# Two mixture-of-experts layers in two halves of the batch, with the state space layer of one half beside the expert tiles of the other

## The chip, the cores and the metric

The kernel runs on one core of one Trainium2 chip. The core has a matrix engine (PE, whose weight loads the profile lists apart as PEld), three engines for the rest of the arithmetic (DVE, ACT, POOL), and SP, which here only issues DMAs. Each engine works through its own instructions in order, and waits where an instruction needs a result that another engine or a DMA has not delivered. The time is device microseconds (us) of one execution.

## The reference

The input `x` holds 4 sequences of 512 tokens with 128 features in f32, 2048 tokens in all. Four layers follow one another, and each is added to its input and normalized over the features:

```
x = layernorm(x + attention(x))    # 16 heads of 8; token t sees t-64 .. t+64
x = layernorm(x + moe0(x))         # shared expert, and the best 2 of 12 experts by softmax weights
x = layernorm(x + ssm(x))          # state space layer
x = layernorm(x + moe1(x))         # the best 2 of 8 experts
```

An expert of `moe0` computes `(a * gelu(g)) @ We2 + be2` with `a, g = split(x @ We1 + be1)`, 384 wide. An expert of `moe1` computes `gelu(x @ w1 + b1) @ w2 + b2`, 512 wide, adds `x`, and applies a layernorm with a gamma and a beta of its own before it is weighted.

The state space layer projects a token to z and x (256 each, 4 heads of 64), B and C (64 each, normalized), and small numbers per head. B and C are turned by a phase that is a running sum over time. Per head a state of 64 x 64 runs over the 512 steps: `h = d[t] * h + input[t]`, with a decay `d` per step and an input made of x and B of this and the step before; `y = C h + D x`; the output is `(y * silu(z)) @ W_out`.

## The kernel before

**Memory and order.** Tiles are 128 tokens (P = 128), so a sequence has NT = 4 of them, and NB = 4 is the number of sequences. Buffers come from pools: a tile with a tag and `bufs=6` has six buffers in turn, and a seventh user waits until the first is free. The order of instructions on each engine is chosen by the framework's scheduler from the program's order and its own estimates; inside `as_written("PE")` PE keeps the order of the program text. Before, only attention stands in such a block.

**Attention** (lines 490 to 800). PE goes through the scores and the products with the values of all four sequences, one after the other. When a sequence's sums are done, a generator, a "chain", takes it on: `attention_out`, then `moe0_shared` (the shared expert, the gates and the top two of 12) and `route`. A part of each chain runs per attention step. The loop goes on until the chains are empty.

**Routing** (lines 303 to 505). The table in DRAM is the core of both expert layers. `route_table` allots one region of NB·T = 2048 rows per expert and fills it with zeros (12 DMAs of 1 MB). `route` gives each token of a sequence its rank within its experts, by matmuls that count, and POOL puts each token's row into the table by indirect DMAs (L363), 8 per sequence and layer, 128 rows each. `route_end` waits for the counts of all four sequences and computes from them which rows and which expert each tile has. With two experts per token and regions that end in a part of a tile, a loop needs a fixed number of tiles:

```
tiles = 2 * NB * T // P + n - 1        # n = 12: 43 tiles; n = 8: 39 tiles
```

`route_regs` loads these numbers into registers for eight tiles at a time. `tiles` (L477) is a pipeline written out by hand; in step t stand the load of tile t+3, the turn of t+1, the up projection of t and the down projection of t−1:

```
for t in range(-3, n + 1):
    if t + 3 < n:          s[t + 3] = load(r, t + 3)
    if 0 <= t + 1 < n:     self.route_turn(r, t + 1, s[t + 1])
    if 0 <= t < n:         up(r, t, s[t])
    if 0 <= t - 1:         down(r, t - 1, s.pop(t - 1))
```

A load is two DMAs on SP and one POOL copy: the tile's rows from the table into `io` (L452, 64 KB; six buffers), the expert's up weights (L453; four buffers), the expert's bias (L456). The turn is a transposition on PE (L462) and a copy on ACT (L463). In `moe0` the up projection is six matmuls (L859), Gelu on ACT (L867) and a product on DVE (L868); the down projection is three matmuls (L471), a DVE copy into `io` (L875) and a store on SP into a second DRAM table, `ys` (L876). In `moe1` POOL adds a vector to the rows (L1266), PE does four matmuls up (L1271), ACT the Gelu (L1274), PE four down, DVE the residual and the layernorm (L1281 to L1289), and SP a store (L1290). A row load, a tile's result and its store share one `io` buffer.

`route_back` gathers, for one sequence, two result rows per token: 8 indirect DMAs on POOL (L498) of 128 rows each. `moe0_back` and `moe1_back` weight and add them and normalize.

**State space layer** (lines 890 to 1230). After the first tile loop, `moe0_back` and `ssm_project` run per sequence, then `ssm_weights` for all 16 tiles together. Time goes in 16 chunks of 128 tokens (4 sequences of 4). `chunk_matrix` computes each chunk's decays between any two of its steps: a DVE product, one f32 matmul of 512 columns (pe, L1126), an exponential on ACT (L1128) and a POOL product (L1129), and scales x three ways on ACT (L1141). `chunk_outputs` adds what the chunk's own inputs give (py) and what the state carries in, and renews the state (pst). `chunk_out` turns y on PE (pyt) and multiplies by W_out. When a sequence is done, its gates and puts for the second layer (`moe1_gates`) run behind the chunks of the next.

**The order of the stages**, from `tile_kernel` (L1314), is: attention, tiles of `moe0`, state space layer, tiles of `moe1`, `moe1_back`. Each stage has pools of its own that close when it ends.

Of the kernel before, what the change touches and what calls it, by code (L numbers as in the profile page):

```python
# [20 lines left out]
D = 128  # L21

# [14 lines left out]
class Kernel:  # L37
# [47 lines left out]
    def consts(self):  # L85
# [48 lines left out]
        nc.vector.tensor_scalar(self.first_row, self.tile_no[:, :16], float(NB * T), None, ALU.mult)  # L134
# [63 lines left out]
    def weights_moe1(self):  # L198
# [6 lines left out]
        for i, name in enumerate(("b2", "gamma")):  # L205
            at = 4 + i * D
            nc.gpsimd.dma_start(
                out=self.u1[:, :, at : at + D], in_=d[name].partition_broadcast(P)
            )
        self.down = self.const.tile([P, NE0 * 3, D], F32, tag="down", name="down1")  # L210
# [91 lines left out]
    def route_table(self):  # L302

        nc = self.nc
        self.table = self.dram.tile([NE0 * NB * T, D], F32, name="table")
        zero = self.const.tile([P, D], F32, tag="zero", name="zero")
        nc.gpsimd.memset(zero, 0.0)
        m = NB * T // P
        for e in range(NE0):
            nc.sync.dma_start(  # L310
                out=self.table[e * NB * T : (e + 1) * NB * T, :].rearrange("(p m) d -> p m d", m=m),
                in_=zero[:, None, :].to_broadcast([P, m, D]),
            )


    def route_start(self, n, name, width, down, bias):
# [3 lines left out]
        tiles = 2 * NB * T // P + n - 1  # L320
# [3 lines left out]
            "n": n, "name": name, "tiles": tiles, "down": down, "bias": bias, "reg": {}, "count": count, "batch": [], "puts": [], "y": {},  # L324
            "ys": self.dram.tile([tiles * P, width], F32, name=f"ys_{name}"),
        }

    def route(self, r, b, x, hots):
# [29 lines left out]
        r["batch"].append((hots, rank))  # L358
        place = self.placed(hots, rank, self.first_row[:, :n], n, "put")
        for i in range(NT):  # L360
            yield
            for k in range(2):
                put = nc.gpsimd.indirect_dma_start(  # L363
                    out=self.table, out_offset=bass.IndirectOffsetOnAxis(ap=place[:, k, i : i + 1], axis=0),
# [20 lines left out]
    def route_end(self, r):  # L385
# [14 lines left out]
        done = self.s2.tile(shape, F32, tag="done", name=f"done{n}", bufs=1)  # L400
# [4 lines left out]
        ex = self.small([P, 64], "ex", 1)[:, :tiles]  # L405
        nc.vector.tensor_reduce(ex, done, AX.X, ALU.add)
        nc.vector.tensor_tensor(done, done, t0[:, None, :].to_broadcast(shape), ALU.mult)
        off = self.small([P, 64], "off", 1)[:, :tiles]
# [3 lines left out]
        table = self.sm.tile([P, 4, 64], I32, tag="table", name="table", bufs=1)  # L412
        nc.vector.scalar_tensor_tensor(
            off, ex, float(NB * T // P), off, ALU.mult, ALU.add
# [3 lines left out]
            table[:, 0, :tiles], off, float(P), float(n * NB * T - P), ALU.mult, ALU.min  # L418
# [5 lines left out]
        r["table"] = table  # L424
# [971 lines left out]
```

## Time and profile before

| | |
|---|---|
| time, median of 14 runs | 840.2 us (836.53 to 848.72) |
| time of the profiled execution | 841.62 us |
| its span, first to last instruction | 839.9 us |
| mean granted PE clock | 0.796 |
| busy: PE | 578.4 us (69%), 3852 matmuls |
| busy: PEld | 402.1 us (48%) |
| busy: DVE | 391.8 us (47%), 1331 instructions |
| busy: ACT | 327.9 us (39%), 861 |
| busy: POOL | 316.4 us (38%), 454 |
| moved by DMA | 68.73 MB, mean 82 GB/s |

Busy times overlap, since the engines run side by side; no engine is busy all the time. The granted clock is the share of full speed at which PE was allowed to run. The span leaves out 1.7 us of the time, around the first and the last instruction.

The chain that ended last, followed back from the last instruction, is by engine: PE 46%, DMA 14%, DVE 12%, ACT 8%, POOL 8%, issue 8%. Its costliest lines are short shares of many stages: `io_b<-table` 5%, `pse` (L687) 4%, `io_a<-table` 4%, `psc` (L658), `table` (L363), `pg` (L859), `py` (L1161), `pe` (L1126) and `ph` (L1271) 3% each. So an average over the span tells little, and the time has to be read stage by stage.

### The profile page before, as it was taken

What the parts mean: (1) busy time and instruction counts of PE and PEld (TensorE: products, weight loads), DVE (VectorE), ACT (ScalarE), POOL (GpSimd) and SP (SyncE); (2) the same over time, 40 slices, a digit from 0 to 9 for tenths busy, and PEclk for the clock granted to TensorE, in tenths of its full rate; (3) what the DMA queues carried; (4) which work ended last, traced back from release to release, by engine and by line L of the source; (5) the groups of instructions that cost most, each with busy time, mean ns of one, the idle gap of its engine ahead of it and who ended that gap; (6) DMA issues with size and microseconds to landing.
All of it is one profiled execution on the core that took longest, in us unless ns stands there. A gap on an engine that the chain in (4) does not pass through costs nothing.

```text
span 839.9 us, 12428 instructions
## 1 busy us (share of the span) xinstructions
PE 578.4 (69%) x3852; PEld 402.1 (48%) x3852; DVE 391.8 (47%) x1331; ACT 327.9 (39%) x861; POOL 316.4 (38%) x454
## 2 busy tenths in 40 slices
PE   5489989599695689889243457886887448888100
PEld 2145444345453488888222334544555348778100
DVE  4375677554334534444343352354454524444245
ACT  1024444244453144444123835463651235555100
POOL 8113433632744400000473524235362343333472
PEclk9599999898787889999765855565875569999655
DMA  6995000000000177777510000000000037666122
GB/s 154 301 283 145 1 2 1 26 1 1 26 2 25 39 213 215 203 203 199 164 51 22 0 1 0 1 0 27 0 26 7 25 119 157 153 162 154 44 63 58
DMA packets 81740, 68.73 MB, mean 82 GB/s; under 512 B 9126, under 2 KB 68539, under 8 KB 81675
## 3 DMA queue, kind: packets, MB, share of 16 engines
q1 hardware_dynamic: 76938, 58.27, 25.9%
q0 software_dynamic: 4736, 9.67, 4.5%
q8 instruction: 32, 0.52, 0.3%
q14 instruction: 34, 0.27, 0.1%
HBM read 44.69 MB, written 23.22 MB: 81 GB/s over the span
## 4 chain that ended last, share of the span: by engine, by line
PE 46%; DMA 14%; DVE 12%; ACT 8%; POOL 8%; issue 8%; SPq 2%; another core or an unknown queue 1%; DVEq 0%; POOLq 0%; ACTq 0%
DMA io_b<-table 5%; PE pse L687 4%; DMA io_a<-table 4%; PE psc L658 3%; POOL table L363 3%; PE pg L859 3%; PE py L1161 3%; PE pe L1126 3%; PE ph L1271 3%; PE pc L710 2%; PE psc L652 2%; PE pa L859 2%; PE py_a L471 2%; PE py_b L471 2%; POOL back_a L498 2%
## 5 line engine op out<-in xcount | busy, mean ns | idle before, releaser
L695 POOL TENSOR_SCALAR_AFFINE_SELECT pt<-pt 128x1024 f32<-128x1024 f32 (+1 forms) x64 | 61.9, 993 | 131.4 <-ACT pt L691 115.8
L691 ACT ACTIVATE pt<-pse 128x384 f32<-128x384 f32 (+1 forms) x128 | 61.0, 550 | 88.3 <-PE pse L687 87.6
L664 DVE TENSOR_REDUCE maxima<-psc 128x2 f32<-128x384 f32 (+1 forms) x128 | 71.5, 616 | 36.3 <-PE psc L658 36.1
L363 POOL DMA_INDIRECT table<-x,put x64 | 64.4, 1007 | 54.6 <-issue 15.2
L868 DVE SCALAR_TENSOR_TENSOR act<-pa,bias_a,ge 128x128 f32<-128x128 f32 x129 | 37.3, 345 | 66.2 <-ACT ge L867 57.7
L687 PE MATMUL pse<-q,k 32*128 32x256 f32 (+1 forms) x512 | 51.1, 393 | 10.2 <-DVE maxima L664 10.2
L652 PE MATMUL psc<-band,ident_bf 128*128 128x384 bf16 (+1 forms) x128 | 40.1, 389 | 20.9 <-DVE wmean L918 13.5
L1274 ACT ACTIVATE hid<-ph,bias_b 128x128 f32<-128x128 f32 x156 | 44.5, 368 | 23.1 <-PE ph L1271 16.6
L687 PEld LDWEIGHTS pse<-q,k 32*128 32x128 f32 x512 | 37.3, 195 | 23.9 <-DVE maxima L664 11.6
L471 PE MATMUL py_b<-down,hid 128*128 x312 | 46.0, 287 | 2.9 <-ACT hid L1274 2.6
L867 ACT ACTIVATE ge<-pg,bias_a 128x128 f32<-128x128 f32 x129 | 38.0, 365 | 20.8 <-PE pg L859 19.9
L456 POOL COPY bias_a<-w_be 128x6 f32 x43 | 7.9, 188 | 97.7 <-DVE act L868 95.4
L471 PEld LDWEIGHTS py_b<-down,hid 128*128 128x128 f32 x312 | 40.5, 191 | 5.8 <-ACT hid L1274 4.8
L1271 PE MATMUL ph<-io_b,wt_b 128*128 128x128 f32 x312 | 43.1, 283 | 0.0
L471 PE MATMUL py_a<-down,act 128*128 x258 | 40.6, 285 | 2.7 <-DVE act L868 1.8
L1271 PEld LDWEIGHTS ph<-io_b,wt_b 128*128 128x128 f32 x312 | 40.7, 202 | 0.1
L222 PE MATMUL tp_xt<-ident,x 128*128 128x128 f32 x48 | 12.1, 362 | 41.1 <-DVE x L250 35.8
L498 POOL DMA_INDIRECT back_a<-ys_a,get x32 | 30.4, 950 | 22.5 <-DMA ys_a<-io_a 13.1
L1281 DVE TENSOR_TENSOR io_b<-py_b,io_b 128x128 f32<-128x128 f32 x39 | 11.3, 290 | 57.6 <-POOL bias_b L456 26.1
L498 POOL DMA_INDIRECT back_b<-ys_b,get x32 | 31.4, 982 | 17.4 <-issue 9.5
L471 PEld LDWEIGHTS py_a<-down,act 128*128 128x128 f32 x258 | 33.8, 191 | 6.4 <-DVE act L868 6.4
L859 PE MATMUL pg<-io_a,wt_a 128*128 128x128 f32 x258 | 36.6, 279 | 0.0
(309 smaller groups left out, 1287.7 us busy)
## 6 DMA issues: line engine op xcount, KB each, us to landing
wt_a<-in_We_dram SPq DMA_DIRECT2D x43, 384.0 KB, 4.0
table<-zero SPq DMA_DIRECT2D x12, 1024.0 KB, 10.4
wt_b<-in_w_dram SPq DMA_DIRECT2D x39, 256.0 KB, 3.6
io_a<-table SPq DMA_DIRECT2D x43, 64.0 KB, 3.3
ys_a<-io_a SPq DMA_DIRECT2D x43, 64.0 KB, 3.0
ys_b<-io_b SPq DMA_DIRECT2D x39, 64.5 KB, 3.3
io_b<-table SPq DMA_DIRECT2D x39, 64.0 KB, 2.7
down<-in_We_dram SPq DMA_DIRECT2D x12, 192.0 KB, 7.3
```

The lines of the kernel that those rows point to most:

```text
L363: put = nc.gpsimd.indirect_dma_start(out=self.table, out_offset=bass.IndirectOffsetOnAxis(ap=place[:, k, i : i + 1], axis=0), in_=x[:, i, ...
L471: nc.tensor.matmul(py[:, :D], lhsT=hidden[:, c * P : (c + 1) * P], rhs=flat[:, bass.ds(r["reg"][t, 2] + c * D, D)], start=c == 0, stop=c = ...
L498: nc.gpsimd.indirect_dma_start(out=back[:, i, k, :], out_offset=None, in_=r["ys"], in_offset=bass.IndirectOffsetOnAxis(ap=place[:, k, i : ...
L652: nc.tensor.matmul(pp, lhsT=self.ident_bf, rhs=self.band[:, None, off : off + w].to_broadcast([P, 2, w]), start=True, stop=False,)
L664: nc.vector.tensor_reduce(self.maxima[b % 2][:, j, at : at + 2], pp, AX.X, ALU.max)
L687: nc.tensor.matmul(pp[:, c], lhsT=s["k"][strip, 2 * cp + c, m * P : (m + 1) * P], rhs=s["q"][strip, c, lo:hi], start=True, stop=True, skip ...
L691: nc.scalar.activation(pt[:, 2 * i : 2 * i + 2, :w], pp, AF.Exp)
L695: nc.gpsimd.affine_select(out=x, in_=x, compare_op=ALU.is_ge, fill=0.0, base=HALF if m == 0 and sign > 0 else 0, pattern=[[0, 2 * G], [sig ...
L859: nc.tensor.matmul(p[:, c * P : (c + 1) * P], lhsT=wt[:, at : at + P], rhs=xt, start=True, stop=True,)
L867: nc.scalar.activation(ge[:, cb], pg[:, cb], AF.Gelu, bias=bias[:, 3 + c : 4 + c])
L1271: nc.tensor.matmul(ph[:, cb], lhsT=s["wt"][:, cb], rhs=s["xt"], start=True, stop=True)
L1274: nc.scalar.activation(hid[:, cb], ph[:, cb], AF.Gelu, bias=s["bias"][:, c : c + 1])
```

## The change

It does five things.

1. **Two halves.** Sequences 0 and 1 form half 0, sequences 2 and 3 half 1 (HB = 2, HC = HB·NT = 8). Each half has a routing table (12 regions of HB·T = 1024 rows; 24 DMAs of 512 KB for the zeros), counts, tile numbers and a result table of its own. So there are four tile loops, with 27 tiles each for the first layer and 23 for the second. `weights_moe1` moves ahead of attention, except for the down weights, which share a buffer with the first layer's and get a function of their own (`weights_down1`).
2. **Other work beside the tiles.** `tiles` takes a generator, and after each step runs `rate` parts of it. To that end `route_back`, `moe0_back`, `moe1_back` and the whole state space layer become generators, and `together` runs two of them in turns. Attention no longer waits for its last chains: it returns what is left of them.
3. **PE's order is written out for the whole kernel**, since everything stands in `as_written("PE")`.
4. **The state space layer is rewritten per half**: two sequences are stacked on 64 + 64 partitions where a state or B and C are concerned. silu(z) is made from a tanh, with the factor one half put into W_out. Each chunk's decays no longer come from a matmul and an exponential: the decays per step are turned, stored into DRAM, and read back broadcast to all partitions (512 KB per chunk step of two sequences, and 2 x 128 KB for the carry); a scan on DVE multiplies them up. Scalings of x move from ACT to POOL, except one. y comes out turned, so `pyt` is gone.
5. **Pools.** `io` moves from six buffers to a pool `wt` with four, which also holds the tiles of the hidden layer (tag `hid`). Pools are opened on two sides of the memory and stay open where their tiles cross stages.

The core of the diff (helpers and constants left out):

```diff
@@ route_table -> route_tables, route_start
-        tiles = 2 * NB * T // P + n - 1
+        tiles = 2 * HB * T // P + n - 1
...
@@ route_load
-        io = self.s2.tile([P, 4 * D + 4], F32, tag="io", name=f"io_{r['name']}{t}", bufs=6)
-        nc.sync.dma_start(out=io[:, :D], in_=self.table[bass.ds(reg[t, 0], P), :])
+        io = self.wt.tile([P, 4 * D + 4], F32, tag="io", name=f"io_{r['name']}{t}")
+        nc.sync.dma_start(out=io[:, :D], in_=r["table"][bass.ds(reg[t, 0], P), :])
@@ tiles
-    def tiles(self, r, load, up, down):
+    def tiles(self, r, load, up, down, beside=iter(()), rate=2):
...
                 down(r, t - 1, s.pop(t - 1))
+            if t >= 0:
+                for _ in range(rate):
+                    next(beside, None)
@@ route_back
+            if i % 2:
+                yield
@@ attention
-        while g < NB * steps + lag or chains:
+        for g in range(-ahead, NB * steps + lag):
...
+        return (part for c in chains for part in c)
@@ moe0_up
-        act = s["act"] = self.s2.tile([P, 3 * P], F32, tag="s2", name=f"act{t}")
+        act = s["act"] = self.wt.tile([P, 4 * P], F32, tag="hid", name=f"act{t}")
@@ chunk_matrix
-        pe = self.bank(f"pe{n}")
-        nc.tensor.matmul(pe, lhsT=self.gt, rhs=r.rearrange("p h t -> p (h t)"), start=True, stop=True)
...
-        nc.scalar.activation(m.rearrange("p h t -> p (h t)"), pe, AF.Exp)
...
+        nc.sync.dma_start(
+            out=dbc,
+            in_=rows[m + i * j : m + (i + 1) * j, :].rearrange("r t -> (r t)").partition_broadcast(P),
+        )
...
+        for k in range(HB):
+            nc.vector.tensor_tensor_scan(
+                w[:, k].rearrange("p h t -> p (h t)"), dbc[:, k * NH1 * P : (k + 1) * NH1 * P],
+                self.prev, 0.0, ALU.mult, ALU.add,
+            )
+        for k in range(HB):
+            nc.gpsimd.tensor_tensor(
+                w[:, k], w[:, k], s["gg"][:, i * HB + k, None, :].to_broadcast([P, NH1, P]), ALU.mult
+            )
@@ chunk_outputs
+                for q, part in heads:
+                    nc.tensor.matmul(
+                        py[k][part, c, :], lhsT=w["xw"][:, k, q, :], rhs=w["m"][:, k, q, :],
+                        start=True, stop=False, skip_group_check=True,
+                    )
...
@@ ssm
+    def ssm(self, h, first, behind):
...
+        x = yield from self.together([self.moe0_back(first, b) for b in bs])
+        yield
+        s, w = {}, {}
+        yield from self.ssm_project(h, x, s)
+        self.ssm_norm(h, s)
+        yield
+        yield from self.ssm_weights(h, s)
+        yield from self.ssm_turn(h, s)
...
+        for i in range(-1, NT + 1):
+            if i + 1 < NT:
+                w[i + 1] = self.chunk_matrix(h, i + 1, s)
+                yield
+            if 0 <= i < NT:
+                self.chunk_outputs(h, i, s, w[i])
+                yield
+            if i >= 1:
+                self.chunk_out(h, i - 1, w.pop(i - 1), x, r)
+                yield
...
+        yield from self.together([behind(b, x[k]) for k, b in enumerate(bs)])
@@ tile_kernel
+    with k.as_written("PE"):
+        side = scope("right", ctx=2, sh=2)
+        main = scope("left", at=2)
+        rest = k.attention(x, lambda b, x: k.moe0_shared(b, x, r0[b // HB]))
+        main.close()
+        ctx.enter_context(scope("left", wt=4, bk=2))
+        k.route_end(r0[0])
+        moe0(0, rest, 1)
+        some(rest)
+        side.close()
+        k.route_end(r0[1])
+        ctx.enter_context(scope("right", sp=1, s2=2))
+        a, b = ssm_half(0), ssm_half(1)
+        moe0(1, a, 2)
+        k.weights_down1()
+        some(b, 9)
+        some(a)
+        moe1(0, b, 2)
+        c = back(0)
+        some(c, 2)
+        some(b)
+        moe1(1, c, 1)
+        some(c)
+        some(back(1))
```

Here `moe0(h, beside, rate)` is the first layer's tile loop of half h, `moe1` the second's; `ssm_half(h)` is a generator that gathers the first layer's results of half h, runs the state space layer and the gates and puts of the second, and ends with its `route_end`; `back(h)` gathers the second layer's results. `some(parts, n)` runs n parts of a generator, or all that are left. So the four loops, called A0, A1, B0 and B1 below, have beside them: A0 the chains that attention left; A1 the state space layer of half 0; B0 that of half 1, of which nine parts stand ahead of its first tile; B1 the gathers and sums of half 0.

## The prediction

> **What bounds the kernel now.** I read the stages first: busy time in stretches cut where the work changes. Columns: stretch, its us, busy us (instructions) of PE, weight loads, DVE, ACT, POOL; granted clock, DMA share, GB/s.
>
> ```profile
> core 0: us, PE busy (x) PEld busy (x) DVE busy (x) ACT busy (x) POOL busy (x), PEclk, DMA share, GB/s
> ...
> 56.00:242.00 186.00, 160.76 (x1437) 89.13 (x1433) 103.35 (x254) 84.69 (x157) 79.78 (x83) 0.91 0.12 34
> 242.00:292.00 50.00, 35.14 (x208) 22.27 (x206) 27.09 (x109) 14.16 (x24) 23.72 (x29) 0.86 0.06 22
> 292.00:412.00 120.00, 101.58 (x817) 95.10 (x817) 46.26 (x172) 50.67 (x173) 10.38 (x43) 0.96 0.70 200
> 412.00:500.00 88.00, 34.08 (x106) 20.82 (x106) 39.29 (x128) 34.68 (x57) 45.43 (x44) 0.66 0.13 33
> 500.00:648.00 148.00, 117.38 (x438) 74.80 (x438) 64.97 (x226) 73.75 (x232) 57.51 (x58) 0.64 0.02 8
> 648.00:680.00 32.00, 10.87 (x50) 8.47 (x50) 13.83 (x79) 5.17 (x8) 16.78 (x20) 0.50 0.10 33
> 680.00:790.00 110.00, 86.51 (x663) 79.62 (x663) 46.65 (x195) 56.61 (x197) 35.12 (x79) 0.93 0.60 143
> 790.00:840.00 50.00, 0.00 (x0) 0.00 (x0) 20.44 (x96) 2.17 (x8) 27.46 (x28) 0.50 0.25 59
> ```
>
> PE sets the pace in attention (its last context matmul ends at 251.5) and in both tile loops (292 to 412, 680 to 790). It is partly idle in attention's tail, in 412 to 500 (gathers, projection, weights), 648 to 680 and all of the last 50 us. Tiles could run there; that is what the change can win.
>
> Next the timeline of a tile loop, for its pace and for a buffer's way round it (start, us, engine, line):
>
> ```profile
> 341.14 0.33 SPq L876 DMA_DIRECT2D ys_a<-io_a  x1
> ...
> 341.79 0.33 SPq L452 DMA_DIRECT2D io_a<-table  x1
> ...
> 343.59 0.33 SPq L876 DMA_DIRECT2D ys_a<-io_a  x1
> ```
>
> From store (341.14) to store (343.59) an undisturbed tile takes 2.45 us; over the stage it is 120/43 = 2.79, in the second loop 110/39 = 2.82. SP issues store, rows, weights in turn and waits in order. The DMA issues, with KB and us to landing:
>
> ```profile
> wt_a<-in_We_dram SPq DMA_DIRECT2D x43, 384.0 KB, 4.0
> ...
> io_a<-table SPq DMA_DIRECT2D x43, 64.0 KB, 3.3
> ys_a<-io_a SPq DMA_DIRECT2D x43, 64.0 KB, 3.0
> ys_b<-io_b SPq DMA_DIRECT2D x39, 64.5 KB, 3.3
> io_b<-table SPq DMA_DIRECT2D x39, 64.0 KB, 2.7
> ```
>
> Last the waits (us, times, longest):
>
> ```profile
> SPq L452 <- DMA ys_a<-io_a: 13.8, 18, 1.6
> ...
> PE tp_xt L222 <- DVE x L250: 35.8, 7, 21.3
> ```
>
> The first: a row load already waits, with six buffers, for the store of the tile whose buffer it takes. The second holds the 21.3 us in which PE stood while POOL gathered the first batch.
>
> **The change, part by part.** A0, A1, B0, B1 are the four new loops (first or second expert layer, half 0 or 1).
>
> *More tiles.* A loop has 2·1024/128 + n − 1: 27 tiles for 12 experts, 23 for 8. That is 54 and 46 instead of 43 and 39: 11·2.79 + 7·2.82 = +50 us of old pace.
>
> *Four io buffers, not six.* The io tile moves to the pool `wt` (bufs=4). The row load of tile t+4 needs the landing of the store of tile t, and stands right behind that store on SP; while it waits, the weights and the next store wait behind it. The down matmuls of t stand in step t+1, the turn of t+4 opens step t+3; so two steps hold one undisturbed step and one round trip: T = (step + DVE + store + issue + load)/2. First layer: step 2.45, DVE to store 0.35, issue 0.1. With the medians 3.0 and 3.3, T = 9.2/2 = 4.6; with the shortest landing of these tiles (1.5, twice) 5.9/2 = 2.95. I take 3.8, the middle: the load meets an emptier queue, the store goes out behind 384 KB of weights. Second layer: step 2.3 (726.13 to 728.40 between two turns), DVE 1.5 (L1281 to L1289), issue 0.1; medians 3.3 and 2.7 give 4.95, the shortest (2.1, twice) 4.05; I take 4.5. With six buffers the sums are divided by four (2.3, 2.5), about a step: that is why they cost little now.
>
> *The state space layer.* PE per half, from rows at full clock: transposes 16 x 0.3 = 4.8, projection 8 x 0.9 + 4 x 1.1 = 11.6, sums over time and decays 3.5, B and C 4.6, chunks 23.5 (state 3 x 1.1, scores 32 x 0.28, own part 16 x 0.28, carry 24 x 0.28), output 4.5, gates 10.5: 63 us. Today 500 to 648 alone is 117 busy, at a clock of 0.64. Gone are the pe matmuls (28.8), the turns of y (8.7) and 16 exponentials (9.5 on ACT). New are 2.75 MB of DMAs a half, on SP between the tiles' (14 us at the 200 GB/s of a tile stage, over 137), and 8 scans of 512 columns on DVE, which no row shows: from 0.71 (a 512-wide multiply) to twice that, 6 to 11 us; DVE has 36 from tiles and some 70 from the layer in 137. I cost both at nothing, under tiles; if that cover is gone, 14 and 11.
>
> *POOL.* Half a layer has 16 gathers, and 16 puts, of 0.95 + 0.30 = 1.27: 20.3 each. PE is now bound to written order throughout, so a transposition that waits for gathered rows holds all tiles behind it; bias copies queue behind gathers too.
>
> *Start.* w_out's scaling stands on DVE before most maxima and waits for a later load: +2.5 (0 to 4). The zeros are the same bytes, long before a put needs them: nothing.
>
> **The sum**, on the profiled run (span 839.9, time 841.6; 0.2% over the median 840.2 of 14 runs):
>
> - Attention ends at 251.5 + 2.5 = 254. A0's first rows are ready, so it starts there, not at 292.
> - A0: 4 free tiles x 2.45 + 23 x 3.8 + 1.2 = 98; 27 us of PE for batches 2 and 3 beside them, mostly in the 1.35 idle of a step: +8. End 360.
> - A1 passes tile 3 only when half 0 is back: store 3.3, gathers 20.3, landing 2.2, sums and layernorm 6: 392.
> - A1's other 24 steps: PE 24 x 2.45 + 63 = 122; ten steps with little beside, 10 x 1.35 = 13; ACT changes tables some 20 times between Gelu and the rest at 1.28, of which 8 (0 to 26) on the path; long steps let the ring catch up, −6 (0 to −13). End 529.
> - Ahead of B0's first tile, PE's order has nine parts of half 1: 32 as above, and 6 of matmuls: 567.
> - B0: 23 x 2.3 + 57 = 110; 12 light steps x 2.2 = 26; +8 −6. End 705.
> - B1: POOL's last puts and the row load, +7; then the 16 gathers of half 0 stand ahead of tile 1's addition on POOL; tile 4 turns some 36 after B0's end: 741. 19 x 4.5 + 1.5 = 87: 828.
> - Half 1 back: DVE and store 4.8, gathers 20.3, then 14.2 as now from the last gather to the end: 867. Outside the span 1.7: **869 us**.
>
> The difference, +27, is +50 of tiles and some +94 of ring (23 + 13 + 26 + 32), less 117 that overlap and the new layer win after three stops of 30 to 38.
>
> After 10.43 us of idling, PE's first eight ph matmuls (683.55) took 2.04 instead of 1.06; after 2.13 us (357.10) six pg took 0.84 as ever. The Trainium skill ("TensorE: Matmul & The Clock Gate", Part 1) has the rule: an idle window of about 3.4 us halves the clock until one busy window has passed. By it each of the three stops costs 1.7 us more, an estimate from that page; the sum would be 874.
>
> **Rivals.**
>
> - *The ring turns at the shortest landings.* T is 2.95 and 4.05: 33 x 0.85 + 31 x 0.45 = 42 less, **827, faster**. For it: DMA is less dense per tile, and such landings occur. Against: the store goes out just behind weights. It decides where store and load together land 0.9 us sooner than I take (64 ring-bound steps, half of it each, is the 27).
> - *The ring does not bind* (2.45 to 2.82 hold): 94 less, 775. Against it: such waits already exist with six buffers.
> - *Written order stops PE.* The layer's matmuls wait for DVE, ACT and POOL (a chunk needs a store to DRAM, 512 KB back, a scan and a POOL product, some 13 us against three steps), tiles wait behind. Two us more on 20 steps: 909.
> - *The overlap does not happen:* stages in turn as now, plus 50 of tiles: 890. It needs A1 and B0 to stand while the layer runs.
>
> **Chances.** Forecast 0.48, shortest landings 0.22, no ring 0.07, written order 0.16, no overlap 0.07; each spreads by some 15 us. A run tells 0.5% from no change (836 to 844). Slower 0.66 (forecast, order, no overlap, less the forecast's low edge), same 0.08, faster 0.26. The range 810 to 915 leaves out the ring-free case and the far ends.
>
> **What would show it.** Row loads of A0 and B1 that wait for stores, at 3.8 and 4.5 us a tile; PE standing 15 to 35 us before the first turn of gathered rows in A1 and before B0, and in B1 behind gathers; A0's first turn near 254; steps of some 5 us beside the layer. Wrong if stores land in under 2 us, or if such steps take 7.

## The result and the profile after

The changed kernel takes **916.9 us** (median of 10 runs, 908.4 to 922.7) against 841.8 us for the kernel before (47 runs): **1.088 times the time, 95% interval 1.085 to 1.092**. The profiled execution has a span of 917.5 us. The forecast was 869 with a range of 810 to 915: slower, as forecast, but by 9% where 3% was forecast, and just outside the range.

First the busy times of each engine by stretch in the changed kernel; columns as in the prediction (stretch, its us, busy us of PE, weight loads, DVE, ACT, POOL, then granted clock, DMA share, GB/s).

```profile
core 0: us, PE busy (x) PEld busy (x) DVE busy (x) ACT busy (x) POOL busy (x), PEclk, DMA share, GB/s
...
259.00:378.00 119.00, 90.61 (x617) 80.71 (x618) 47.55 (x190) 42.21 (x123) 22.24 (x45) 0.89 0.41 117
378.00:417.00 39.00, 18.54 (x89) 15.01 (x89) 13.59 (x60) 9.62 (x24) 16.27 (x21) 0.65 0.41 118
417.00:542.00 125.00, 99.22 (x705) 82.89 (x703) 78.83 (x257) 66.12 (x162) 46.26 (x53) 0.89 0.37 112
542.00:599.00 57.00, 18.30 (x70) 13.79 (x71) 16.90 (x68) 7.54 (x17) 24.38 (x29) 0.58 0.33 93
599.00:715.00 116.00, 89.74 (x624) 75.24 (x623) 81.54 (x276) 68.54 (x178) 52.43 (x65) 0.88 0.30 87
715.00:738.00 23.00, 6.89 (x40) 5.64 (x39) 4.20 (x24) 2.56 (x7) 14.00 (x17) 0.62 0.26 84
738.00:783.00 45.00, 21.84 (x121) 20.51 (x120) 16.34 (x77) 17.70 (x43) 21.35 (x30) 0.65 0.28 69
783.00:872.00 89.00, 48.92 (x281) 47.07 (x280) 20.82 (x89) 23.57 (x84) 14.22 (x33) 0.77 0.30 82
872.00:917.50 45.50, 5.22 (x37) 5.02 (x35) 13.26 (x63) 4.77 (x13) 15.35 (x16) 0.58 0.16 40
```

A0 runs from 259 to 378, A1 with the first layer half beside it from 417 to 542, B0 from 599 to 715, B1 from 738 to 877 (at 738 B0's last tile is turned, at 745 B1's first). The three stops between them are there. But look at the line 783 to 872: nothing stands beside B1's tiles there, and PE is busy for 49 of 89 us, at a clock of 0.77. The loops of the kernel before had 87 to 102 busy of 110 to 120.

What PE waits for (engine, line, releaser: us in all, times, longest):

```profile
PE pxs_b L469 <- DMA io_b<-table: 81.3, 21, 12.8
PE tp_xt L227 <- DVE x L255: 35.8, 5, 25.8
PE pxs_a L469 <- DMA io_a<-table: 32.4, 20, 3.9
```

The first and the third are turns that wait for their rows, 114 us in all. One round of it, in B1's free stretch (start, us, engine, line):

```profile
839.82 0.33 PE L469 MATMUL pxs_b<-ident,io_b 128*128 128x128 f32 x1 [4.81 <-DMA io_b<-table]
839.99 1.75 PE L1358 MATMUL ph<-io_b,wt_b 128*128 128x128 f32 x8
...
841.53 1.91 PE L478 MATMUL py_b<-down,hid 128*128 x8
...
844.85 2.36 SPq L1377 DMA_DIRECT2D ys_b<-io_b  x2
...
847.47 0.34 SPq L459 DMA_DIRECT2D io_b<-table  x1
...
850.18 0.33 PE L469 MATMUL pxs_b<-ident,io_b 128*128 128x128 f32 x1 [4.71 <-DMA io_b<-table]
```

This is the ring of the forecast: turn, up and down projection, DVE, store (5.0 us), from the store to the next row load (2.6), landing of the rows (2.7), together 10.4 us for two tiles. The 2.6 is a little more than the store's own landing: the line at 844.85 is two stores, the second one the next tile's, and the row load follows 0.3 us behind that one on SP. By the trace the first store had landed by 846.7. The turns come in pairs, a long and a short distance in alternation. Over seven whole pairs (798.0 to 870.8) they are 5.20 us apart on average, as the ring has it; the forecast took 4.5. (The 5.36 that some expectations below quote is the mean from 790.4 on, which counts an eighth long distance without its short one.)

### The profile page after: what moved, and what is told of

Read it like the earlier page. It is cut to its first block, busy times and chain, and to the rows that moved or that the text cites. A ratio compares the mean times of both kernels' runs of the same rounds, so it can differ in the third digit from the quotient of the medians.

```text
span 917.5 us, 13795 instructions
## 1 busy us (share of the span) xinstructions
PE 606.5 (66%) x4240; PEld 455.1 (50%) x4240; DVE 436.3 (48%) x1457; ACT 337.2 (37%) x822; POOL 333.4 (36%) x478
## 5 line engine op out<-in xcount | busy, mean ns | idle before, releaser
L469 PE MATMUL pxs_b<-ident,io_b 128*128 128x128 f32 x46 | 17.1, 376 | 81.6 <-DMA io_b<-table 81.3
L1358 PE MATMUL ph<-io_b,wt_b 128*128 128x128 f32 x368 | 68.0, 346 | 0.6 <-ACT io_b L470 0.6
L478 PE MATMUL py_b<-down,hid 128*128 x368 | 63.6, 330 | 4.5 <-ACT hid L1361 4.5
L1358 PEld LDWEIGHTS ph<-io_b,wt_b 128*128 128x128 f32 x368 | 64.0, 261 | 1.3 <-ACT io_b L470 0.8
L478 PEld LDWEIGHTS py_b<-down,hid 128*128 128x128 f32 x368 | 60.2, 247 | 5.2 <-ACT hid L1361 5.2
L1353 POOL TENSOR_TENSOR io_b<-io_b,bias_b 128x128 f32<-128x128 f32 x46 | 23.0, 504 | 93.7 <-PE pxs_b L469 77.6
L478 PEld LDWEIGHTS py_a<-down,act 128*128 128x128 f32 x324 | 48.2, 220 | 17.7 <-DVE act L880 16.7
L470 ACT COPY io_a<-pxs_a 128x128 f32<-128x128 f32 x54 | 14.2, 266 | 109.0 <-PE pxs_a L469 81.3
L871 PE MATMUL pg<-io_a,wt_a 128*128 128x128 f32 x324 | 53.8, 310 | 0.3 <-ACT io_a L470 0.3
L871 PE MATMUL pa<-io_a,wt_a 128*128 128x128 f32 x324 | 52.9, 307 | 0.0
```

The lines of the kernel that those rows point to most:

```text
L478: nc.tensor.matmul(py[:, :D], lhsT=hidden[:, c * P : (c + 1) * P], rhs=flat[:, bass.ds(r["reg"][t, 2] + c * D, D)], start=c == 0, stop=c = ...
L871: nc.tensor.matmul(p[:, c * P : (c + 1) * P], lhsT=wt[:, at : at + P], rhs=xt, start=True, stop=True,)
L1358: nc.tensor.matmul(ph[:, cb], lhsT=s["wt"][:, cb], rhs=s["xt"], start=True, stop=True)
```

## The experiments

Every ratio is to the kernel before on the same chip (818 to 836 us there); to compare with the forecast, take a ratio times 841.8 us. "B1" is the mean distance of the turns in B1's free stretch (over whole pairs where they come in pairs), "A0" the time from A0's first turn to half 0's first gather, both from one profiled execution.

| run | ratio (95%) | B1, us | A0, us |
|---|---|---|---|
| the change | 1.088 (1.085 to 1.092) | 5.2 | 124 |
| split | 0.983 (0.972 to 0.994) | 3.3 | 94 |
| io6 | 0.974 (0.962 to 0.986) | 2.9 | 97 |
| io8 | 0.961 (0.953 to 0.968) | 2.0 | 94 |
| before_io4 | 1.112 (1.102 to 1.122) | | |
| before_io9 | 0.985 (0.976 to 0.994) | | |
| free | 1.037 (1.018 to 1.056) | 3.8 | 115 |
| turn_last | 1.034 (1.024 to 1.045) | 3.9 | 113 |
| warm | 1.075 (1.058 to 1.092) | 4.9 | 121 |
| io6_free | 0.969 (0.955 to 0.983) | 2.7 | 95 |
| bias_dve | 1.074 (1.065 to 1.083) | 5.2 | 123 |
| io6_turns | 1.068 (1.034 to 1.102) | | |
| later | 0.976 (0.957 to 0.995) | | |
| swap | 0.977 (0.968 to 0.987) | | |
| io8_rate3 | 0.967 (0.959 to 0.975) | | |
| io8_free_bias | 0.960 (0.954 to 0.967) | | |

### Is it the ring? split, io6, io8

```diff
# split
-        io = self.wt.tile([P, 4 * D + 4], F32, tag="io", ...)
+        io = self.wt.tile([P, 2 * D], F32, tag="io", ...)
+        yo = self.wt.tile([P, D + 4], F32, tag="yo", ...)   # result, stored from here
# io6
+        io = self.wt.tile([P, 3 * D + 4], F32, tag="io", ..., bufs=6)
# io8: the result takes the place of the turned rows
+        io = self.wt.tile([P, 2 * D + 4], F32, tag="io", ..., bufs=8)
```

> The changed kernel with one edit: a tile's result gets a buffer of its own (four of them), apart from its rows, so that the load of rows of tile t+4 no longer waits for the store of tile t. Bytes, matmuls and their order stay the same. Theory (the ring of four buffers costs most of the loss: PE idles 114 us before turns that wait for row loads): A0 falls from 4.4 to some 3.2 us a tile, the free part of B1 from 5.3 to under 3, and the whole from 917 to 825 to 860 us. Rival (the written order of PE holds the tiles behind the state space layer and POOL, and the waits for rows are only where that shows): the same waits reappear before other matmuls, and the time stays above 890.

> The changed kernel with six buffers in place of four for the tile that holds rows, turned rows and result (cut to the columns in use, so that they fit). Store and load stay in one ring, but the ring has four steps of slack instead of two. Theory of the ring: nearly all of the gain of the run with separate buffers, 830 to 865 us, since (step + DVE + store + issue + load) of some 9.5 us is then shared by four. Rival (the store and the load on SP's queue themselves are slow, whatever the number of buffers): less than a third of that gain.

> The changed kernel with eight smaller buffers in place of four for a tile's rows, turned rows and result (the result takes the place of the turned rows, which are dead by then, so the eight take the room of the four). Theory (the ring is gone with six already in the changed kernel, where most steps are long because of the work beside them): within 1.2% of io6, 0.962 to 0.985 of the kernel before. Rival (the ring of six still binds as it did a little in the kernel before): 0.955 or less.

With nothing changed but which buffer waits for what, the kernel goes from 9% slower to 2 to 4% faster than before. The ring costs (1.088 − 0.961) x 841.8 = 108 us (101 to 115, from the two intervals). Some 12 of these may be stalls of another kind in the change (shown under bias_dve): warm and bias_dve, which keep the four buffers and the written order, lie at 1.075 and 1.074, and from there to io8 it is 96 us. In split PE's waits for rows are not all gone (51 us before `pxs_b`, from 81), and its B1, 3.3 us, misses the "under 3" of its theory, while its time, 827 us on the forecast's scale, fits it. In io8 the waits nearly are gone. PE's waits in io8:

```profile
PE tp_xt L227 <- DVE x L255: 53.3, 8, 36.0
...
PE pxs_b L469 <- DMA io_b<-table: 12.8, 3, 9.8
```

io6 gained more than the theory said (820 us on the forecast's scale, not 830 to 865). io8 lies between its theory (0.962 to 0.985) and its rival (0.955 or less), and its interval overlaps with io6's; B1's pace, 2.0 us against 2.9, shows that six buffers still held the tiles there.

### The same edit in the kernel before: before_io4, before_io9

```diff
-        io = self.s2.tile(..., bufs=6)
+        io = self.s2.tile(..., bufs=4)      # before_io9: bufs=9
```

> The kernel before with one number changed: four buffers for that tile, not six. It has full loops, no halves, nothing beside the tiles. Theory of the ring: the first loop goes from 2.79 to between 3.6 and 4.6 us a tile, the second from 2.82 to between 4.5 and 5.3 (with PE's clock down after each wait), together +100 to +150: 940 to 990 us. Rival (four buffers suffice where nothing else runs, and the loss in the changed kernel comes from the work beside the tiles): under 870.

> The kernel before with nine buffers for that tile, not six: a control for the comparison of io6 with before. Theory (with six the ring is shared by four steps, 9.3/4 = 2.3 to 2.5 us, just under a step, and row loads waited 13.8 us for stores in all): at most 1.5% faster, so that the gain of io6 is the overlap's and not a better ring's. Rival (the tile loops of the kernel before are still bound by the ring, at 2.55 and 2.49 us a tile): 2.5% or more, and the overlap with six buffers gains nothing over a loop with enough buffers.

Four buffers alone, without halves and without anything beside the tiles, make the kernel before 11% slower: its turns come 3.47 and 3.68 us apart in the two loops, where it had 2.55 and 2.49. That is a little under the expected 3.6 and 4.5, and the time, 936 us on the forecast's scale, a little under the expected 940; the free order of PE there may be why (free, below). Nine buffers give 1.5%, at the bound that the theory set: turns 2.45 and 2.26 us apart, some 4 us in the first loop and 9 in the second. So a fair comparison of the overlap is io8 with before_io9: 0.961 against 0.985.

### Why the ring is dearer in the changed kernel: free, turn_last, io6_free

```diff
# free, io6_free: as_written("PE") around attention alone
# turn_last
+            if 0 <= t < n: up(r, t, s[t])
+            if 0 <= t - 1: down(r, t - 1, s.pop(t - 1))
             if 0 <= t + 1 < n: self.route_turn(r, t + 1, s[t + 1])
-            if 0 <= t < n: ...
-            if 0 <= t - 1: ...
```

> The changed kernel, still with four buffers, but PE's order is written out for attention alone, as in the kernel before; the framework's scheduler chooses it from there on. Theory (with four buffers the ring sets the pace, whatever the order; a free order can only put a down projection further ahead and so shorten the ring by at most a step of 1 to 2 us per two tiles): 5.4 us a tile in the second half of B1 falls towards the 3.7 that the kernel before has with four buffers, A0 stays near 4.4, and the whole lies at 0.98 to 1.06 of the kernel before. Rival (written order as such is what costs: PE stands behind the state space layer's matmuls): at or below 0.98 of the kernel before, since the tiles then fill what the layer leaves.

> The changed kernel with four buffers and PE's order written out as it is; only three statements of a tile step change places: the turn of tile t+1 is written behind the up projection of t and the down projection of t-1 instead of ahead of them. Theory (the ring is so dear because in the written order the turn's wait for its rows also holds up t and down t-1, whose store would free the next buffer; behind them the same ring of about 9.5 us spans three tiles instead of two): B1 5.4 to 3.0 to 3.6 us a tile, A0 4.4 to 3.3 to 3.8, and the whole at 0.98 to 1.02 of the kernel before instead of 1.088. Rival (the ring has its length whatever the order, and the free order won by other moves, beside the layer): B1 stays above 4.8 and the whole above 1.06.

> Six buffers, and PE's order written out for attention alone. This asks what the written order costs when the ring is out of the way. Theory (it cost 5% with four buffers because it lengthened the ring; without the ring PE waits for the layer's data in either order): within 2% of io6, 0.955 to 0.993 of the kernel before. Rival (the forecast's third rival: tiles stand behind the layer's matmuls in the written order, two us or more on twenty steps): 4% or more under io6, below 0.94.

With four buffers a free order wins 5% and takes B1 to the 3.8 us that the kernel before has with four. Moving one statement in the written order does the same. In the lines above the reason can be seen: the turn at 839.82 waits for rows, and the up and down projections behind it wait too, though they need none of these rows; the stores of these tiles are what the next row loads wait for, or stand behind on SP. turn_last fell short of its theory (3.9 us, not 3.0 to 3.6), so it doesn't show that the ring then spans three tiles; that the turn's place costs some 5% it does show (4% against warm: 8 us in A0 and 26 in B1, by the table under bias_dve). With six buffers the written order costs nothing that can be measured (0.969 against 0.974): the forecast's third rival, PE standing behind the layer's matmuls, falls.

### The clock in the ring: warm

```diff
+            if r["name"] == "b1" and t >= 5 and t % 2 == 0:
+                for _ in range(7): matmul(idle, lhsT=self.ident, rhs=self.prev)   # thrown away
```

> The changed kernel with work added that is thrown away: in B1, from tile 5 on, seven matmuls of 512 columns after each second down projection, where PE idles 4.7 to 5 us for the next rows. Theory (the idling lowers PE's granted clock, so that the next up projection takes 1.9 us instead of 1.06 and the down projection 1.9 instead of 1.06, and both stand in the ring): the turns of B1, 5.36 us apart now, come 4.5 to 5.0 us apart, and the kernel gains 5 to 15 us though PE does some 27 us more. Rival (the clock does not matter to the ring, or the added matmuls end too late): no gain, or a loss of 5 to 25 us.

Granted clock (the column behind POOL's busy time) in B1's free stretch, first the changed kernel, then warm:

```profile
784.00:872.00 88.00, 48.42 (x278) 46.86 (x279) 19.83 (x84) 22.82 (x81) 14.22 (x33) 0.77 0.30 82
```

```profile
784.00:832.00 48.00, 48.00 (x233) 31.01 (x232) 11.84 (x50) 13.24 (x49) 7.70 (x18) 1.00 0.26 76
```

One round of warm:

```profile
802.51 0.27 PE L469 MATMUL pxs_b<-ident,io_b 128*128 128x128 f32 x1
802.62 1.06 PE L1362 MATMUL ph<-io_b,wt_b 128*128 128x128 f32 x8
...
803.52 1.06 PE L478 MATMUL py_b<-down,hid 128*128 x8
...
805.98 2.22 SPq L1381 DMA_DIRECT2D ys_b<-io_b  x2
806.31 6.17 PE L500 MATMUL idle<-prevs,ident 128*128 128x512 f32 x14
808.47 0.34 SPq L459 DMA_DIRECT2D io_b<-table  x1
...
812.32 0.27 PE L469 MATMUL pxs_b<-ident,io_b 128*128 128x128 f32 x1
```

From turn to store it takes 3.5 us where the change took 5.0: the two projections run at 1.06 us each instead of 1.75 and 1.91. That is the clock's price in the ring, 1.5 us for two tiles. The tiles come 4.90 us apart and not 5.20, some 4 us over 14 tiles. It is less than the 0.8 a tile that the clock costs, because PE no longer waits for rows at all in this stretch: those of the turn at 812.3 had landed by 810.6, and it stands behind the matmuls that are thrown away (6.2 us), which now set the pace. B1 as a whole is no shorter, 133 us from half 0's second gathers to half 1's in both, and the time's own interval (1.058 to 1.092) doesn't separate warm from the change. So the theory's pace came, its gain of 5 to 15 us is not shown, and it is the time from turn to store that carries the cause.

### POOL's queue: bias_dve

```diff
-        nc.gpsimd.tensor_copy(bias, ...)      # and the addition to the rows in moe1_up
+        nc.vector.tensor_copy(bias, ...)
```

> The changed kernel with the copies of the experts' biases, and the addition of a vector to the rows in the second layer, moved from POOL to DVE, so that they no longer stand behind gathers and puts. Theory (three places where tiles wait for a bias behind 16 gathers or 16 puts on POOL: 8 us at the start of A1, some 14 at the end of A1, 10 to 20 at the ends of B0 and the start of B1): 917 falls by 20 to 45. Rival (those stops are set by the gathered rows themselves, which come no earlier): within 10 of 917.

It wins 1.4%, 12 us (4 to 20): under what the theory wanted, over its rival's bound by a little. But the change was timed on another chip, and the stages of the profiles say that the gain is not the biases'. The marks are A0's first turn and the first instructions of POOL's blocks of 16 gathers or puts; each row goes from one mark to the next (us):

| stage | the change | warm | bias_dve | turn_last | io8 |
|---|---|---|---|---|---|
| A0's first turn to half 0's gathers | 124 | 121 | 123 | 113 | 94 |
| to half 0's puts (layer in A1) | 149 | 143 | 141 | 144 | 144 |
| to half 1's gathers (stop) | 38 | 29 | 29 | 29 | 29 |
| to half 1's puts (layer in B0) | 142 | 140 | 141 | 141 | 131 |
| to half 0's second gathers (stop) | 38 | 28 | 28 | 28 | 29 |
| to half 1's second gathers (B1) | 133 | 133 | 133 | 106 | 71 |

warm has the biases on POOL and four buffers, and it differs from the change in B1 alone; yet its stops are as short as those of bias_dve. So the biases' place costs the stops nothing that these profiles show. What the change has more than the others is this. POOL at the end of A1:

```profile
L463 POOL COPY bias_a<-w_be x54: 186/191/1150, 256.4 to 527.1; 128x6 f32 x54
...
550.61 0.96 POOL L370 DMA_INDIRECT table<-x,put  x1 [0.31 <-issue]
...
551.62 0.75 POOL L463 COPY bias_b<-u 128x260 f32 x2
...
569.64 1.01 POOL L509 DMA_INDIRECT back_a<-ys_a,get  x1 [3.98 <-issue]
```

(The first line lists all copies of A1's and A0's biases: count, shortest, median and longest in ns, first and last start.) PE and ACT in the same stretch:

```profile
539.48 0.30 PE L469 MATMUL pxs_a<-ident,io_a 128*128 128x128 f32 x1 [1.41 <-DMA io_a<-table]
...
542.75 0.60 PE L522 MATMUL tp_gt<-ident,e_g 128*8 128x128 f32 x4
...
547.77 0.27 ACT L470 COPY io_a<-pxs_a 128x128 f32<-128x128 f32 x1 [9.65 <-issue]
...
554.16 0.89 ACT L879 ACTIVATE ge<-pg,bias_a 128x128 f32<-128x128 f32 x3 [6.13 <-remote]
...
554.93 0.56 ACT L526 COPY gt<-tp_gt 8x512 f32<-8x512 f32 x1
...
555.54 2.07 PE L1341 MATMUL pbeta<-w_beta,gt 8*128 8x128 f32 x8 [12.19 <-ACT gt L526]
...
592.48 2.39 PE L227 MATMUL tp_xt<-ident,x 128*128 128x128 f32 x8 [25.77 <-DVE x L255]
```

The 16 puts of half 0 run from 531 to 551.6; the last bias copy of A1 began ahead of them, at 527.1. ACT copies rows at 547.8 that PE had turned at 539.5, and the Gelu behind that copy starts 6 us later; the profile names no engine and no DMA of this core as what they waited for ("issue", "remote"). PE, in its written order, waits 12 us for the gates' copy, which stands behind that Gelu on ACT. Stalls of the same look stand at the end of half 0's gathers (ACT, 397 and 405) and of B0 (ACT and DVE, 720 to 732). No other run of a changed kernel shows a "remote" wait of over 3 us; the kernel before has one, of 3.1 us, next to a 10 us stall of ACT at 449. What they are stays open, and so does how many of the change's other runs have them. In the change's profile they are some 10 us of each stop.

Of the 29 us that all the others have, 20 are the puts, ahead of the gathers on POOL. The other 9 come from SP's order, as io8 shows:

```profile
510.79 0.29 DVE L887 COPY io_a<-py_a 128x128 f32<-128x128 f32 x1 [0.38 <-PE py_a L478]
...
516.63 0.34 SPq L459 DMA_DIRECT2D io_b<-table  x1
...
520.23 1.61 SPq L888 DMA_DIRECT2D ys_a<-io_a  x2
...
524.14 1.01 POOL L509 DMA_INDIRECT back_a<-ys_a,get  x1 [7.31 <-issue]
```

The result of A1's last tile is there at 511, but its store stands on SP behind the row loads of B0's first tiles, and these wait for the puts, which end at 515. Half 1's gathers read what that store writes. No run puts these stores ahead of the row loads.

### What the overlap is worth, and what bounds it: io6_turns, io8_rate3, later, swap, io8_free_bias

```diff
# io6_turns: the four loops without anything beside them (A1 shown), and six buffers
-        moe0(1, a, 2)
+        moe0(1, iter(()), 2)
+        some(a); some(b)
# io8_rate3
-        moe0(1, a, 2)
+        moe0(1, a, 3)
# later: gathers ahead of the loop, the layer's first matmul some six tiles into it
+        some(a, 6); a = later(12, a)          # and the same for b
# swap: as later, and
-        c = back(0); some(c, 2); some(b)
+        some(b); c = later(4, back(0))
```

> Six buffers as before in io6, but nothing beside the tiles: the chains that attention leaves run before A0, the whole layer of half 0 and then of half 1 between A1 and B0, and the gathers of both halves behind B1. This prices the overlap. Theory (with the ring out of the way the overlap is what pays: A1 and B0 hide 45 to 55 us of tiles each behind the layer): 0.974 of the kernel before becomes 1.06 to 1.14. Rival (tiles and layer only stretch one another, so that overlapping them is worth little): under 1.02.

> io8 with three parts of the layer after each tile of A1 and B0, not two, so that the layer is spread over some 15 tiles and not 22. Theory (the layer is a chain: each part waits for the one before on DVE, ACT, POOL or a DMA, about 2.5 us a part whatever stands beside it, and so tiles beside it are nearly free): A1 and B0 keep their length within 5 us each if tiles that are left over run at 2.1 to 2.5 us, and the kernel stays within 1.5% of io8. Rival (PE's sum sets those loops): the kernel does not move either, but steps then grow by less than the part added, under 1 us. The steps tell them apart: theory 6.5 us or more a step beside the layer, rival under 5.5, against 5.0 with two parts.

> Six buffers, the biases' copies and the addition on DVE, and the gathers of a half written ahead of the loop beside which its layer runs, with twelve empty parts behind them, so that PE's order has the first six tiles of A1 and of B0 ahead of the first transposition of gathered rows (now tile 3 in A1, none in B0). Theory (PE stands 26 us in A1 and some 30 before B0 for gathered rows, and tiles can fill half of that): 15 to 35 us under io6, 0.93 to 0.955 of the kernel before. Rival (the tiles are only moved, and the layer's end, which B0's and B1's rows wait for, comes later by as much): within 1% of io6.

> The kernel called later, with one more move: the gathers of half 0 for the end stand behind the puts of half 1 instead of ahead of them, beside B1 from its fourth step on. Theory (after the layer of half 1 the end is set by a chain of puts, 20 us, B1, 55 to 65 us, and the last gathers, and in later 16 gathers, 20 us, stood ahead of the puts on POOL): 12 to 25 us less, 0.945 to 0.962 of the kernel before. Rival (the gathers then stand in B1's way, or the rows are awaited for another reason): within 1% of later.

> io8 with PE's order written out for attention alone and the biases' copies and the addition on DVE. Theory (what is left is the chain of halves: gathers 20 us, layer some 100, puts 20, gathers 20, and neither the order nor the queue of biases lengthens it by much): 0.95 to 0.975 of the kernel before. Rival (order and POOL's queue each hide behind the other in the single runs, and both gone give back most of the 45 us): 0.94 or less.

The overlap is worth 0.094 of the time, 79 us (49 to 110, from the two intervals): without it, six buffers and two halves take 1.068. How much of it is free shows in the time from the layer's first transposition of gathered rows to that of its gates, for half 0 and half 1: 78 and 90 us with nothing beside it (io6_turns), 105 and 93 with tiles after each two parts (io8), 84 and 91 with tiles after each three (io8_rate3). So in io8 18 tiles in B0 cost the layer 3 us, and 17 in A1 27 us, though alone such tiles take some 2.4 and 2.7 each (medians of io6_turns). A part of that is the clock and not only waits that tiles fill: in these stretches the layer alone has a granted clock of 0.69 and 0.56, and beside tiles 0.88 and 0.89, so that its own matmuls are faster there. No run takes the two apart; on the chain that ended last in io8, half 1's chunks (604 to 637) are 92% PE's work. For io8_rate3, steps in the layer's chunks grew to 8.3 us (four steps from 412.4), as the theory of a chain had it (6.5 or more); but A1's layer ended 21 us earlier with 11 tiles beside it, not 17, so there tiles are not free. The time is io8's either way, since tiles that are left over run behind the layer. later and swap move PE's waits without shortening the kernel: in later, POOL runs puts and gathers 32 in a row (488 to 528 and 648 to 689), and B1 starts late instead; swap brings B1's first turn forward from 693 to 686, and B1 then takes 76 us where it took 60. io8_free_bias says the same: neither the order nor the biases hold what is left. By its marks, what is left in io8 is a chain of halves (no run takes a piece of it away): six blocks of 16 indirect DMAs at 20 us, the layer at 105 and 93, A0 and B1.

## Why the prediction was wrong

The direction and the mechanism were right: four buffers make a ring of two steps, and without the ring the overlap wins. Three steps of the sum failed: A0's step (3.8, measured 4.4), B1's step (4.5, measured 5.2, since the clock's price inside the ring was left out), and the ends of A1 and B0, where the puts and what waits for them were priced at 3 and 7 us. By marks that both have (forecast, measured, io8):

| | forecast | the change | io8 |
|---|---|---|---|
| A0's first turn | 254 | 259 | 258 |
| half 0's first gather | 363 | 382 | 352 |
| half 1's first gather | 532 | 570 | 524 |
| first gather of the last 16 | 833 | 882 | 755 |
| end of the span | 867 | 917.5 | 790.8 |

(The forecast's gathers are its ends of A0 and A1 and 3.3 for the store, and of B1 and 4.8.) The 50 us are 5 at the start, 14 in A0, 19 in A1 and the stops around it, 11 in B0 and B1 together, 1 at the end. Two of these are small only because misses of both signs meet, which is luck. In A1: +5 until gathered rows are turned, −12 in its steps, +25 from their end to half 1's gathers. In B0 and B1: −6 and −22 up to the end of B0's steps, +19 from there to B1's tile 4 (715 to 770, forecast 36 us), +20 for the tiles behind it.

- **The ring, in all.** Forecast 94 us, measured 108, or some 96 without the change's stalls. But it is not where it was forecast. From the change to io8 the table under bias_dve has 30 us in A0 (forecast 23), 5 in A1 (13), 11 in B0 (26) and 62 in B1 (32); that the total came near is luck. The rivals "shortest landings" and "the ring does not bind" fall with split and io6. (For the first, 64 half-steps of 0.9 us are 29 us, not 27; nothing hangs on it.)
- **"I take 3.8, the middle" (A0).** Measured 4.4 a tile with the chains beside it. A pair of turns between 305.9 and 314.6 has 3.4 us from turn to store, 3.4 until the row load, 1.9 until the turn: T = 4.35. The rows landed sooner than the median of 3.3 that the forecast started from, the store no sooner than its 3.0: together 5.3, where a step of 3.8 leaves 4.7. From turn to store it took 3.4, where the forecast had 2.8. Besides, +8 for the chains of sequences 2 and 3 was too little: where the ring is gone their 27 us of PE come in full (io8: A0 has 86.5 of 94 us busy).
- **"Second layer: step 2.3" (B1).** The two landings, 5.1 in the sum, took no more than was forecast (2.6 + 2.7 in the round above), in part by luck, as the 2.6 is the wait behind the next tile's store. But turn, projections, DVE and issue took 5.0 and not 3.9, as PE is slower after each wait of 4.4 to 4.9 us: 1.7 to 1.9 us for each projection where it has 1.06 at a granted clock of 1.00 (warm: 3.5 us in all). T = 10.4/2 = 5.2. The forecast held the clock's price ready and put it on three stops only, outside its sum. The Trainium skill describes this too ("TensorE: Matmul & The Clock Gate", "HAM oscillation — how this bites in real kernels"): a loop whose step ends in a wait for a DMA that is longer than the idle window starts every step cold. The trace agrees (clock 0.77, and 1.00 in warm, where the wait is filled).
- **The ring's length: "two steps hold one step and one round trip".** Right, but half of the reason was missed: not the buffers alone but also the turn's place ahead of the projections make it two steps (free and turn_last: some 5%).
- **The end of A1.** The forecast let half 1's gathers follow A1's last store, 3 us after A1's steps. Measured are 28 (542 to 570). The 16 puts of half 0 stand between, 20 us on POOL in every version, then some 9 us of stores behind row loads on SP, and in the change some 10 of stalls. For B1 the forecast had the last puts and the row load as +7.
- **What was priced too high:** steps beside the layer. Up to the holds at their ends, A1's steps took 125 us (417 to 542), not 137, and B0's 116 (599 to 715), not 138. The layer from its first transposition to its gates takes 102 and 104 us there, little else than the 105 and 93 of io8: the ring hides in it. That made up for part of the misses.
- **"I cost both at nothing" (DMAs and scans of the layer).** Nearly held. In the stretches above DVE is busy for at most 70% (82 of 116 us). On the chain that ended last in io8, which the profile follows back to half 1's gathers, stands no scan, but one load of the layer with 4.4 us (599.1). The scans took 1.80 us each in the change (1.54 in io8), 14 a half, over the bounds of 6 to 11.
- **Extra tiles.** 18 tiles at the median steps of io6_turns (2.2 and 2.7 us in the first layer's loops, 2.4 and 3.1 in the second's) are some 46 us; the forecast had 50.

What stays open: the forecast's sum without the ring, 775, is 33 us under io8's 808 (0.9605 x 841.8). By the marks of io8's profile the parts are +4 at the start, +8 in A0, +16 in A1 and the stops around it, −12 in B0 and B1, +2 at the end; the rest is that io8 ran on a chip where the kernel before takes 822 us. No run takes them apart.

## What to carry to other kernels

Count what a buffer goes through before it is free (fill, use, store, landing), divide by the steps between two of its uses, and compare with the step: a buffer that holds both a tile's input and its output puts a store and a load into one ring, and here eight smaller buffers in the room of four were worth 11 to 13% of the kernel's time before. In an order written out by hand, an instruction that can wait for a DMA belongs behind those that don't need it. And before tiles are laid beside a layer, ask whether the layer is a chain of waits or is bound by the engine that the tiles want: here 18 tiles cost one half's layer 3 us and 17 cost the other's 27, and the overlap was worth 79 us (49 to 110), about what the ring took away. Last, a block of work can hold up another through a third queue: here stores that were ready stood behind loads that waited for puts.

## What the runs showed of the hardware

PE's granted clock falls within a loop whose waits are under 5 us each (0.77); the eight matmuls behind such a wait take 1.7 to 1.9 us instead of 1.06. Seven matmuls of 512 columns (6.2 us in all) behind each second down projection hold it at 1.00. A scan over 128 x 512 f32 on DVE takes 1.80 us in the change (1.22 to 2.19), where a multiplication of that size in the kernel before took 0.71. Sixteen indirect DMAs of 128 rows take POOL 20 us, each 0.96 with 0.30 between.
